# All additions of the last layer's pieces behind a block's edges, sums and shares in one PSUM tile, groups of four

## The chip, the cores and the metric

The kernel runs on one core of a Trainium2 chip, as one launch. The metric is the device time of one execution in microseconds (us). The core has five engines that run their own instruction streams and wait for each other through semaphores: TensorE (PE, matrix products; loads of its stationary operand appear as PEld), VectorE (DVE), ScalarE (ACT), GpSimd (POOL) and SyncE (SP, which here only issues transfers). Products land in PSUM, which has eight banks; all other tiles are in SBUF.

## The reference

The input is x (4096 x 128) and a sparse, symmetric pattern of edges in a dense matrix adj (4096 x 4096, float32, some ten entries a row, the diagonal among them, weights from 0.05 to 1). Four graph layers follow each other, each with a residual and a layer norm. The change concerns the last two:

```python
# layer 2: attention over the edges, 4 heads of 32 features
h_prime = (x @ weight.T).reshape(n, heads, f_out)
alpha_src = jnp.sum(h_prime * att_src, axis=-1)
alpha_dst = jnp.sum(h_prime * att_dst, axis=-1)
C = alpha_src[None, :, :] + alpha_dst[:, None, :]
adj_t = adj_matrix.T[..., None]
tau = adj_t * jnp.exp(jnp.maximum(0.2 * C, C))
tau_sum = jnp.sum(tau, axis=1, keepdims=True)
att_weights = tau / tau_sum
z = jnp.einsum('mnh,nhf->mhf', adj_t * att_weights, h_prime)
x = _layernorm(x + z.reshape(n, heads * f_out) + bias)
# layer 3: mean over the edges
deg = jnp.clip(jnp.sum(adj, axis=1, keepdims=True), 1.0)
h_neigh = adj @ h / deg
x = _layernorm(x + h @ W_self + h_neigh @ W_neigh)
```

## The kernel before

The layers ahead of these end with products of adj with dense blocks (L397, L687, L1685); beside them DVE and POOL build lists of each row's edges. `sparse_layers` (L1406) holds the two last layers. The 4096 rows are 32 blocks of 128 (NT = 32); adj is loaded as chunks of 1 MB, and columns of a product come in 8 stretches of 512 (NB = 8).

**Layer 2 for block t.** `gathers` (L1492) fetches the neighbours' rows from a table in DRAM with nine indirect transfers that POOL issues (L1497), two blocks ahead, into `got` (four buffers). Behind every second one stands a small POOL instruction, `pause` (L1391, L1393); two of the four read something and so wait: the second gather's reads `rd` of block t-2, the sixth's a column of the sum that was last added. `targets` (L1507) makes three small products that spread values of the target rows over the edges, in a PSUM tile `u` (shares, told[t]), one block ahead. `edges` (L1514) is DVE's work: `into` (L1523), scores (L1526 to L1529), an exponential on ACT (L1530), the weights (L1531, L1532, the latter written into `u`), the weighted rows `gw` (L1533) and the sum over the six near edges `here` (L1535). `sums` (L1538) adds up on PE in a PSUM tile `so`: three products with `into` and one of `here` with the identity (L1541, L1542). `divide` (L1545) divides by the sum of weights (`rd`, `z`) and adds to x; `turn` (L1555) transposes the block on PE and takes its statistics on DVE.

**Layer 3** is turned around: as soon as a group of n blocks has left layer 2, `layer3_rows` (L1562) makes its rows times both weight matrices (copy `oT` on ACT, n products L1575, then y and x scaled on ACT), and `layer3_product` (L1598) multiplies these rows with their part of adj: 8 stretches, each a product of n matmuls ("pieces") in a PSUM tile `pp`, to be added to the running sum `acc3` in SBUF by `add_up` (L1610; a copy on ACT for the first group, else an addition on DVE, L1618). The matrix part comes through `columns` (L1590) in 1 MB loads on SP's queue; five buffers hold them. `layer3_end` (L1620) does the last group together with the final norm and the store.

**The order** of PE, DVE, ACT and POOL is written out by hand: the loop over t near the end calls these functions in turn, `one(chains)` takes a step of `layer3_rows`, `one(pieces)` one matmul of `layer3_product`, and `multiply(n)` (L1667) up to n of these, with an `add_up` ahead of each, or, with held=True, without additions until two products wait. Each engine executes its instructions in exactly the order in which they are recorded.

PSUM before: two banks for `u`, three for `pp`, two for `px` (transposes, L1575), one for `so`. Groups are of 1, 1, fourteen times 2, 1 and 1 blocks.

Of the kernel before, what the change touches and what calls it, by code (L numbers as in the profile page):

```python
# [11 lines left out]
F32 = mybir.dt.float32  # L12
# [4 lines left out]
AF = mybir.ActivationFunctionType  # L17
ALU = mybir.AluOpType
AX = mybir.AxisListType
PSUM = bass.MemoryType.PSUM  # L20

P = 128
IB = 512
TB = IB // P
# [11 lines left out]
QT = 3  # L36
# [7 lines left out]
def adj_resnorm_d4(ctx: ExitStack, tc: tile.TileContext, x_in, xT_in, adj, adjT, w0g, w0gT, a0, w1a, b1a,  # L44
# [7 lines left out]
    nc = tc.nc  # L52
    N, F = x_in.shape
    NT = N // P
# [4 lines left out]
    H = att_src.shape[1]  # L59
# [11 lines left out]
    x = state.tile([P, NT, F], F32, name="x")  # L71
# [14 lines left out]
    eps = const.tile([P, 1], F32, name="eps")  # L86
# [1317 lines left out]
            nc.vector.tensor_tensor(flag, pb, flag0, ALU.add)  # L1404

    def sparse_layers(enter, lists, w, h0T):  # L1406
        psum, ps_p, ps_x, ps_so = [enter(name=n, bufs=b, space=PSUM) for n, b in (("ps_u", 2), ("ps_p", 3), ("ps_x", 2), ("ps_so", 1))]
        l2 = enter(name="l2", bufs=2)
        spread, table = lists.spread, lists.table
        lists.psum = psum  # L1410
        E = NEAR + QT
        W = 3 * H + 1
# [10 lines left out]
        def inverse(s, v):  # L1423
            nc.scalar.activation(s, v, AF.Sqrt, bias=eps)
            nc.vector.reciprocal(s, s)
# [63 lines left out]
        got, told, wide = {}, {}, {}  # L1489
        warm = small.tile([P, 1], F32, name="warm")  # L1490
# [16 lines left out]
        def targets(t):  # L1507
            if t < NT:
                at = wide[t // TB][:, t % TB]
                told[t] = psum.tile([P, QT * W + E * H], F32, name="u")  # L1510
                for j in range(QT):
                    nc.tensor.matmul(told[t][:, j * W:(j + 1) * W], at[:, j * P:(j + 1) * P], dst[:, t], start=True, stop=True)

        def edges(t):  # L1514

            g, u = got.pop(t), told.pop(t)
            d = u[:, 0:QT * W].rearrange("p (j s) -> p j s", s=W)
            wt = u[:, QT * W:].rearrange("p (j h) -> p j h", h=H)
            a = lists.value[:, t][:, :, None].to_broadcast([P, E, H])
            gw = l2.tile([P, E + 1, F + H], F32, name="gw")  # L1520
            nc.scalar.copy(gw[:, E, :], own[:, t, :])
            into = l2.tile([P, QT, P], F32, name="into")
            nc.vector.tensor_tensor(into, lists.iota[:, None, :].to_broadcast([P, QT, P]),  # L1523
                                    d[:, :, 3 * H:W].to_broadcast([P, QT, P]), ALU.is_equal)
            e = l2.tile([P, E, H], F32, name="score")
            nc.vector.tensor_reduce(e[:, 0:QT], d[:, :, 0:3 * H].rearrange("p j (s h) -> p j h s", s=3), AX.X, ALU.add)  # L1526
            nc.vector.tensor_tensor(e[:, QT:], g[:, QT:, F:F + H], near[:, t, :][:, None, :].to_broadcast([P, NEAR, H]), ALU.add)
            nc.vector.tensor_tensor(e[:, 0:QT], e[:, 0:QT], g[:, 0:QT, F:F + H], ALU.add)
            nc.vector.scalar_tensor_tensor(e, e, ALPHA, e, op0=ALU.mult, op1=ALU.max)  # L1529
            nc.scalar.activation(e, e, AF.Exp)  # L1530
            nc.vector.tensor_tensor(gw[:, 0:E, F:F + H], e, a, ALU.mult)  # L1531
            nc.vector.tensor_tensor(wt, gw[:, 0:E, F:F + H], a, ALU.mult)  # L1532
            nc.vector.tensor_tensor(heads(gw[:, 0:E, 0:F]), heads(g[:, :, 0:F]), wt[:, :, :, None].to_broadcast([P, E, H, FO]), ALU.mult)  # L1533
            here = l2.tile([P, F + H], F32, name="here")
            nc.vector.tensor_reduce(here, gw[:, QT:, :].rearrange("p j f -> p f j"), AX.X, ALU.add)  # L1535
            return into, gw, here

        def sums(into, gw, here):  # L1538
            so = ps_so.tile([P, F + H], F32, name="so")
            for j in range(QT):  # L1540
                nc.tensor.matmul(so, into[:, j, :], gw[:, j, :], start=j == 0, stop=False)  # L1541
            nc.tensor.matmul(so, ident, here, start=False, stop=True)  # L1542
            return so
# [18 lines left out]
        def layer3_rows(t0, n):  # L1562

            s = small.tile([P, n], F32, name="rstd2")
            xb = l2.tile([P, n, P], F32, name="oT")
            nc.scalar.copy(xb, turned.pop(t0))
            inverse(s, mv[:, t0:t0 + n, 1])
            yield
            qs = []
            for k0 in range(0, n, 2):  # L1570
                m = min(2, n - k0)
                q = ps_x.tile([P, m, 2, F], F32, name="px")
                qs += [(k0 + k, q[:, k]) for k in range(m)]
                for k in range(m):
                    nc.tensor.matmul(q[:, k].rearrange("p s f -> p (s f)"), xb[:, k0 + k, :],  # L1575
                                     W3.rearrange("p s f -> p (s f)"), start=True, stop=True)
            yield
            for k, q in qs:
                nc.scalar.activation(y[:, t0 + k, 0:F - 1], q[:, 0, 0:F - 1], AF.Copy, scale=s[:, k:k + 1])  # L1579
            for k, q in qs:  # L1580
                if n == 1:
                    nc.vector.tensor_scalar_mul(x[:, t0 + k, :], q[:, 1, :], s[:, k:k + 1])
                else:
                    nc.scalar.activation(x[:, t0 + k, :], q[:, 1, :], AF.Copy, scale=s[:, k:k + 1])
            nc.scalar.activation(warm, eps, AF.Exp)
            yield

        adds = deque()
# [9 lines left out]
        def layer3_product(t0, n):  # L1598

            for ib in range(NB):  # L1600
                if ib % (TB // n) == 0:
                    a = columns(t0, n, ib)
                p = ps_p.tile([P, IB], F32, name="pp")
                for k in range(n):
                    nc.tensor.matmul(p, y[:, t0 + k, :], a[:, ib % (TB // n), k, :], start=k == 0, stop=k == n - 1)  # L1605
                    if k == n - 1:
                        adds.append((t0, p, slice(ib * IB, (ib + 1) * IB)))
                    yield

        def add_up():  # L1610
            while adds:
                t0, p, blk = adds.popleft()
                nonlocal summed
                summed = acc3[:, blk.start:blk.start + 1]
                if t0 == 0:
                    nc.scalar.copy(acc3[:, blk], p)
                else:
                    nc.vector.tensor_add(acc3[:, blk], p, acc3[:, blk])  # L1618
# [36 lines left out]
        with tc.manual_schedule(engines={mybir.EngineType.PE, mybir.EngineType.DVE, mybir.EngineType.Activation,  # L1655
# [3 lines left out]
            def one(queue, n=1):  # L1659
                while queue and n:  # L1660
                    r = next(queue[0], queue)
                    if r is not queue:
                        n -= 1
                    else:
                        queue.popleft()

            def multiply(n, held=False):  # L1667
                for _ in range(n):
                    if not held:
                        add_up()  # L1670
                    elif len(adds) > 1:
                        break
                    one(pieces)

            def begin(t0, n):
                pieces.append(layer3_product(t0, n))
                return
                yield

            for ib in range(NB):  # L1680
                p = ps_p.tile([P, IB], F32, name="pp")
# [15 lines left out]
            nc.vector.memset(y[:, :, F - 1], 1.0)  # L1697
            lists.check()
            targets(0)
            sizes = [1, 1] + [2] * 14 + [1, 1]  # L1700
            groups = [(sum(sizes[:i]), n) for i, n in enumerate(sizes)]
            of = {t: g for g in groups for t in range(g[0], sum(g))}
            for t in range(NT):
                t0, n = of[t]
                if t % TB == 1:
                    load_spread(t // TB + 1)
                targets(t + 1)
                multiply(2)
                one(chains)
                multiply(1)  # L1710
                add_up()
                multiply(4, held=True)
                made = edges(t)
                add_up()
                if t == t0 + n - 1:
                    nc.scalar.activation(warm, eps, AF.Sqrt)
                so = sums(*made)
                multiply(2, held=True)
                rd = divide(t, so)
                turn(t, t0, n)  # L1720
                if t == t0 + n - 1:
                    chains.append(layer3_rows(t0, n))
                    if t < NT - 1:
                        chains.append(begin(t0, n))
                for _ in range(3):
                    one(chains)
                    multiply(1)
                behind = {1: rd}
                if summed is not None:
                    behind[5] = summed  # L1730
                gathers(t + 2, behind)
            while chains or pieces:
                one(chains)
                multiply(2)
            add_up()
# [46 lines left out]
```

## Time and profile before

| | |
|---|---|
| median of three runs | 1786.98 us (1784.92 to 1793.05) |
| the profiled execution | 1788.24 us, its span 1786.4 us |
| granted TensorE clock, mean over the span | 0.957 |
| PE busy | 1645.1 us, 92% of the span |
| DVE busy | 1091.3 us, 61% |
| POOL busy | 436.2 us, 24% |
| ACT busy | 371.7 us, 21% |
| additions to acc3 on DVE (L1618) | 128, 682 ns each |
| pieces on PE (L1605) | 496 records, two for each matmul |
| gathers on POOL (L1497) | 288, 962 ns each |

Shares of the whole span hide the stages: up to about 1330 us the dense products keep PE full; the two last layers take from there to 1750 us, and the final norm the rest. The granted clock is the mean share of full speed that PE got in a stretch. In the order of time a line gives the start and the duration in us, the engine, the line, the operation and its tiles, xN for N merged instructions, and in brackets how long the engine had stood idle and what ended it. "issue" means that it waited for nothing that the profile shows. Durations are of one profiled execution.

### The profile page before, as it was taken

How to read it: one execution, taken by the hardware profiler on the slowest of the kernel's cores; microseconds unless marked ns; L12 is line 12 of the kernel's file. 1: busy time of each engine (PE TensorE's matmuls, PEld its weight loads, DVE VectorE, ACT ScalarE, POOL GpSimd, SP SyncE). 2: the span in 40 equal slices, each digit the busy share in tenths (PEclk: the TensorE clock that was granted, in tenths of full speed). 3: DMA queues.
4: the chain of work that ended last, by engine and by line, in shares of the span. 5: the costliest groups of instructions: out<-in, count | busy, mean ns of one | idle time of the engine just before them, and what ended most of it. 6: DMA issues, size and time to landing. Idle time of an engine off the chain costs nothing.

```text
span 1786.4 us, 15851 instructions
## 1 busy us (share of the span) xinstructions
PE 1645.1 (92%) x4968; PEld 771.8 (43%) x4968; DVE 1091.3 (61%) x3066; ACT 371.7 (21%) x664; POOL 436.2 (24%) x636
## 2 busy tenths in 40 slices
PE   7999999999999999999999999999965788887884
PEld 3344445444444444444444444444432333443443
DVE  6655447888877876767966421232334667666665
ACT  5865501100000110101000000121222221222224
POOL 0000000000000000000463543000008877777752
PEclk8999999999999999999999999999986899889898
DMA  9987665688888567766877778888874677667772
GB/s 383 367 322 288 234 222 180 245 328 299 294 303 304 212 242 259 252 213 245 291 258 284 272 273 296 298 296 291 300 203 109 203 246 242 212 214 226 233 185 64
DMA packets 95936, 455.05 MB, mean 255 GB/s; under 512 B 15585, under 2 KB 25826, under 8 KB 52962
## 3 DMA queue, kind: packets, MB, share of 16 engines
q1 hardware_dynamic: 74256, 422.93, 67.2%
q0 software_dynamic: 12288, 19.54, 4.4%
q10 hardware_dynamic: 9298, 11.47, 1.9%
q8 instruction: 41, 0.67, 0.1%
q14 instruction: 53, 0.43, 0.1%
HBM read 446.48 MB, written 7.41 MB: 254 GB/s over the span
## 4 chain that ended last, share of the span: by engine, by line
PE 77%; DVE 10%; DMA 5%; ACT 3%; issue 3%; POOL 2%; ACTq 0%; DVEq 0%; POOLq 0%; SPq 0%
PE pacc L687 35%; PE pp L1685 12%; PE pacc L397 11%; PE pp L1605 6%; DMA chunk<-in_adjT 2%; DVE gw L1533 2%; POOL got L1497 2%; PE pmm L716 2%; DVE here L1535 2%; PE px L1575 1%; PE pden L385 1%; DVE acc L1618 1%; PE ptr L397 1%; DMA got<-table,source 1%; PE ptr L155 1%
## 5 line engine op out<-in xcount | busy, mean ns | idle before, releaser
L1497 POOL DMA_INDIRECT got<-table,source x288 | 277.0, 962 | 311.7 <-issue 307.2
L1386 POOL DMA_INDIRECT value<-in_adjT,where x96 | 99.5, 1037 | 638.1 <-DVE bad L1314 526.4
L1605 PE MATMUL pp<-chunk,xT 128*128 128x512 f32 x496 | 247.3, 647 | 6.1 <-ACT xT L1579 5.9
L687 PE MATMUL pacc<-chunk,v 128*128 128x512 f32 x512 | 225.4, 595 | 0.0
L1685 PE MATMUL pp<-chunk,w 128*128 128x512 f32 x512 | 224.6, 592 | 0.0
L687 PE MATMUL pacc<-chunk,t 128*128 128x512 f32 x512 | 223.5, 592 | 0.0
L687 PE MATMUL pacc<-chunk,x 128*128 128x512 f32 x512 | 222.1, 592 | 0.0
L397 PE MATMUL pacc<-chunk,hw 128*128 128x512 f32 x408 | 188.0, 605 | 2.1 <-DVE numT L425 1.3
L1274 DVE MAX8 top<-chunk 128x8 f32<-128x512 f32 x224 | 143.9, 679 | 57.4 <-DMA chunk<-in_adjT 57.4
L1275 DVE FIND_INDEX8 at<-top,chunk 128x8 uint16<-128x512 f32 x224 | 151.1, 685 | 0.0
L687 PEld LDWEIGHTS pacc<-chunk,v 128*128 128x128 f32 x512 | 95.9, 190 | 117.0 <-issue 117.0
L687 PEld LDWEIGHTS pacc<-chunk,x 128*128 128x128 f32 x512 | 96.2, 190 | 115.8 <-issue 115.8
L687 PEld LDWEIGHTS pacc<-chunk,t 128*128 128x128 f32 x512 | 96.1, 190 | 115.3 <-issue 115.3
L1605 PEld LDWEIGHTS pp<-chunk,xT 128*128 128x128 f32 x496 | 98.2, 210 | 108.9 <-issue 90.7
L1685 PEld LDWEIGHTS pp<-chunk,w 128*128 128x128 f32 x512 | 95.1, 190 | 109.3 <-issue 108.6
L1618 DVE TENSOR_TENSOR acc<-pp,acc 128x512 f32<-128x512 f32 x128 | 84.8, 682 | 48.4 <-PE pp L1605 48.2
L397 PEld LDWEIGHTS pacc<-chunk,hw 128*128 128x128 f32 x408 | 74.5, 190 | 92.2 <-issue 86.0
L328 DVE TENSOR_SCALAR pos<-chunk 128x2048 bf16<-128x2048 f32 x66 | 80.4, 1222 | 48.1 <-DMA chunk<-in_adjT 43.5
L369 ACT ACTIVATE junk<-chunk 128x2048 fp8e4<-128x2048 f32 x51 | 97.4, 1910 | 26.9 <-DMA chunk<-in_adjT 26.5
L1249 POOL IOTA i<- 128x384 int32 (+3 forms) x4 | 1.0, 260 | 333.1 <-PE pden L385 319.1
L1541 PE MATMUL so<-gw,into 128*128 128x132 f32 x192 | 30.1, 295 | 34.3 <-DVE gw L1533 34.1
L1535 DVE TENSOR_REDUCE here<-gw 128x132 f32<-128x924 f32 x32 | 58.4, 1825 | 1.1
(305 smaller groups left out, 1649.1 us busy)
## 6 DMA issues: line engine op xcount, KB each, us to landing
chunk<-in_adjT SPq DMA_DIRECT2D x386, 1024.0 KB, 4.9
keep<-in_adjT SPq DMA_DIRECT2D x13, 1024.0 KB, 8.1
spread<-spread ACTq DMA_DIRECT2D x16, 384.0 KB, 4.1
got<-table,source POOLq DMA_INDIRECT x288
table<-rows ACTq DMA_DIRECT2D x8, 264.0 KB, 6.5
xT<-in_xT ACTq DMA_DIRECT2D x8, 256.0 KB, 8.1
out<-o SPq DMA_DIRECT2D x8, 256.0 KB, 2.3
value<-in_adjT,where POOLq DMA_INDIRECT x96
```

Of the source, the lines that this page charges most:

```text
L328: r = nc.vector.tensor_scalar(pos, a, 0.0, None, op0=ALU.is_gt)
L369: nc.scalar.activation(junk, a, AF.Relu, scale=-1.0, accum_out=bad[:, n:n + 1], saturate=False)
L397: in_order(nc.tensor.matmul(p, hw[:, j * TB + k, :], a[:, k, :], start=first and k == 0, stop=last and k == TB - 1))
L687: nc.tensor.matmul(p, stationary(c * TB + k), a[:, k, :], start=n == 0 and k == 0, stop=n == NB - 1 and k == TB - 1)
L1274: nc.vector.max(self.top[:, t, ib, :], row)
L1275: nc.vector.max_index(self.at[:, t, ib, :], self.top[:, t, ib, :], row)
L1386: pin(nc.gpsimd.indirect_dma_start(self.value[:, c * TB + k, j:j + 1], None, flat, bass.IndirectOffsetOnAxis(ap=self.where[:, c * TB + k, ...
L1497: nc.gpsimd.indirect_dma_start(got[t][:, j, :], None, table, bass.IndirectOffsetOnAxis(ap=lists.source[:, t, j:j + 1], axis=0))
L1535: nc.vector.tensor_reduce(here, gw[:, QT:, :].rearrange("p j f -> p f j"), AX.X, ALU.add)
L1605: nc.tensor.matmul(p, y[:, t0 + k, :], a[:, ib % (TB // n), k, :], start=k == 0, stop=k == n - 1)
L1618: nc.vector.tensor_add(acc3[:, blk], p, acc3[:, blk])
L1685: nc.tensor.matmul(p, w[:, c * TB + k, :], a[:, k, :], start=c == 0 and k == 0, stop=c == NB - 1 and k == TB - 1)
```

## The change

The additions to acc3 no longer stand between the pieces. `multiply` issues up to n matmuls and stops when four products wait for their addition; `add_up` is called once a block, right behind `edges`, so that DVE adds up to four products in a row between `here` and `rd`. To hold four waiting products `pp` gets four banks; the bank comes from `so`, whose sums now lie in the same PSUM tile as the shares of the block (`u`, behind them). Groups become 1, 1, 2, four times 4, five times 2, 1 and 1. Six pieces stand ahead of the edges of a block and two behind its sums. In `layer3_rows` the load of the exponential's table (`warm` with Exp) moves ahead of the products of L1575, the product of the group is queued as soon as its y is there (before by a chain of its own, `begin`), and the scaling of x follows a step later, always on ACT. After the last block the rest of the pieces run with an `add_up` ahead of each two.

```diff
--- before.py
+++ after.py
@@ -1404,7 +1404,7 @@
             nc.vector.tensor_tensor(flag, pb, flag0, ALU.add)
 
     def sparse_layers(enter, lists, w, h0T):
-        psum, ps_p, ps_x, ps_so = [enter(name=n, bufs=b, space=PSUM) for n, b in (("ps_u", 2), ("ps_p", 3), ("ps_x", 2), ("ps_so", 1))]
+        psum, ps_p, ps_x = [enter(name=n, bufs=b, space=PSUM) for n, b in (("ps_u", 2), ("ps_p", 4), ("ps_x", 2))]
         l2 = enter(name="l2", bufs=2)
         spread, table = lists.spread, lists.table
         lists.psum = psum
@@ -1507,7 +1507,7 @@
         def targets(t):
             if t < NT:
                 at = wide[t // TB][:, t % TB]
-                told[t] = psum.tile([P, QT * W + E * H], F32, name="u")
+                told[t] = psum.tile([P, QT * W + E * H + F + H], F32, name="u")
                 for j in range(QT):
                     nc.tensor.matmul(told[t][:, j * W:(j + 1) * W], at[:, j * P:(j + 1) * P], dst[:, t], start=True, stop=True)
 
@@ -1515,7 +1515,7 @@
 
             g, u = got.pop(t), told.pop(t)
             d = u[:, 0:QT * W].rearrange("p (j s) -> p j s", s=W)
-            wt = u[:, QT * W:].rearrange("p (j h) -> p j h", h=H)
+            wt = u[:, QT * W:QT * W + E * H].rearrange("p (j h) -> p j h", h=H)
             a = lists.value[:, t][:, :, None].to_broadcast([P, E, H])
             gw = l2.tile([P, E + 1, F + H], F32, name="gw")
             nc.scalar.copy(gw[:, E, :], own[:, t, :])
@@ -1533,10 +1533,9 @@
             nc.vector.tensor_tensor(heads(gw[:, 0:E, 0:F]), heads(g[:, :, 0:F]), wt[:, :, :, None].to_broadcast([P, E, H, FO]), ALU.mult)
             here = l2.tile([P, F + H], F32, name="here")
             nc.vector.tensor_reduce(here, gw[:, QT:, :].rearrange("p j f -> p f j"), AX.X, ALU.add)
-            return into, gw, here
-
-        def sums(into, gw, here):
-            so = ps_so.tile([P, F + H], F32, name="so")
+            return u[:, QT * W + E * H:], into, gw, here
+
+        def sums(so, into, gw, here):
             for j in range(QT):
                 nc.tensor.matmul(so, into[:, j, :], gw[:, j, :], start=j == 0, stop=False)
             nc.tensor.matmul(so, ident, here, start=False, stop=True)
@@ -1565,6 +1564,7 @@
             xb = l2.tile([P, n, P], F32, name="oT")
             nc.scalar.copy(xb, turned.pop(t0))
             inverse(s, mv[:, t0:t0 + n, 1])
+            nc.scalar.activation(warm, eps, AF.Exp)
             yield
             qs = []
             for k0 in range(0, n, 2):
@@ -1577,12 +1577,11 @@
             yield
             for k, q in qs:
                 nc.scalar.activation(y[:, t0 + k, 0:F - 1], q[:, 0, 0:F - 1], AF.Copy, scale=s[:, k:k + 1])
+            if t0 + n < NT:
+                pieces.append(layer3_product(t0, n))
+                yield
             for k, q in qs:
-                if n == 1:
-                    nc.vector.tensor_scalar_mul(x[:, t0 + k, :], q[:, 1, :], s[:, k:k + 1])
-                else:
-                    nc.scalar.activation(x[:, t0 + k, :], q[:, 1, :], AF.Copy, scale=s[:, k:k + 1])
-            nc.scalar.activation(warm, eps, AF.Exp)
+                nc.scalar.activation(x[:, t0 + k, :], q[:, 1, :], AF.Copy, scale=s[:, k:k + 1])
             yield
 
         adds = deque()
@@ -1664,18 +1663,11 @@
                     else:
                         queue.popleft()
 
-            def multiply(n, held=False):
+            def multiply(n):
                 for _ in range(n):
-                    if not held:
-                        add_up()
-                    elif len(adds) > 1:
+                    if len(adds) > 3:
                         break
                     one(pieces)
-
-            def begin(t0, n):
-                pieces.append(layer3_product(t0, n))
-                return
-                yield
 
             for ib in range(NB):
                 p = ps_p.tile([P, IB], F32, name="pp")
@@ -1697,7 +1689,7 @@
             nc.vector.memset(y[:, :, F - 1], 1.0)
             lists.check()
             targets(0)
-            sizes = [1, 1] + [2] * 14 + [1, 1]
+            sizes = [1, 1, 2] + [TB] * 4 + [2] * 5 + [1, 1]
             groups = [(sum(sizes[:i]), n) for i, n in enumerate(sizes)]
             of = {t: g for g in groups for t in range(g[0], sum(g))}
             for t in range(NT):
@@ -1705,23 +1697,18 @@
                 if t % TB == 1:
                     load_spread(t // TB + 1)
                 targets(t + 1)
-                multiply(2)
-                one(chains)
-                multiply(1)
-                add_up()
-                multiply(4, held=True)
+                multiply(6)
                 made = edges(t)
                 add_up()
+                one(chains)
                 if t == t0 + n - 1:
                     nc.scalar.activation(warm, eps, AF.Sqrt)
                 so = sums(*made)
-                multiply(2, held=True)
+                multiply(2)
                 rd = divide(t, so)
                 turn(t, t0, n)
                 if t == t0 + n - 1:
                     chains.append(layer3_rows(t0, n))
-                    if t < NT - 1:
-                        chains.append(begin(t0, n))
                 for _ in range(3):
                     one(chains)
                     multiply(1)
@@ -1730,6 +1717,7 @@
                     behind[5] = summed
                 gathers(t + 2, behind)
             while chains or pieces:
+                add_up()
                 one(chains)
                 multiply(2)
             add_up()
```

## The prediction

> **What bounds the kernel now.** I read the page first for the share of each engine, then the stretches of 50 us for the stage that the change touches, then the chain that ended last in a part of that stage, and last the order of time on POOL and DVE. The stage runs from the first gather at 1336.2 us to the last addition at 1750.1 us: 32 blocks, each with 9 gathers on POOL, DVE's work on the edges, PE's sums, and a part of the last layer's products.
>
> ```profile
> 1486.00:1536.00 50.00, 41.64 (x121) 20.66 (x120) 33.09 (x74) 10.86 (x28) 38.07 (x53) 0.86 0.71 224
> 1536.00:1586.00 50.00, 41.61 (x122) 20.22 (x121) 33.70 (x76) 10.86 (x28) 38.04 (x53) 0.90 0.72 227
> 1586.00:1636.00 50.00, 41.03 (x123) 20.01 (x122) 33.74 (x76) 10.86 (x28) 37.92 (x52) 0.90 0.72 228
> ```
>
> After the length come busy time of PE, PE's weight loads, DVE, ACT and POOL, the granted clock and the DMA share. No engine is full: PE 83%, POOL 76% and DVE 67%. So the engines wait for each other in turn, and the chain says how.
>
> ```profile
> 1570.81 0.38 ACT xT L1579
> 1571.23 5.67 PE pp L1605 x8
> 1576.89 0.68 PE so L1541 x6
> 1577.57 0.48 PE so L1542 x2
> 1578.06 1.72 PE pp L1605 x4
> 1579.89 2.58 PE pp L1605 x6
> 1582.52 2.69 PE pp L1605 x6
> 1585.85 0.54 DVE into L1523
> ```
>
> The reader is to see that the edges of a block (from L1523) start only when DVE has added products that PE has just made. POOL is not in this chain; it waits for it:
>
> ```profile
> 1678.85 0.32 POOL L1393 TENSOR_TENSOR idle<-rd,idle 128x1 f32<-128x1 f32 x1
> 1692.06 0.19 POOL L1393 TENSOR_TENSOR idle<-rd,idle 128x1 f32<-128x1 f32 x1 [1.44 <-DVE rd L1548]
> 1704.03 0.31 POOL L1393 TENSOR_TENSOR idle<-rd,idle 128x1 f32<-128x1 f32 x1
> 1717.23 0.19 POOL L1393 TENSOR_TENSOR idle<-rd,idle 128x1 f32<-128x1 f32 x1 [1.43 <-DVE rd L1548]
> 1574.49 0.94 POOL L1497 DMA_INDIRECT got<-table,source  x1 [0.30 <-issue]
> 1575.81 0.98 POOL L1497 DMA_INDIRECT got<-table,source  x1 [0.15 <-issue]
> ```
>
> Two blocks take 1717.23 - 1692.06 = 25.2 us, 12.6 each. POOL alone needs less: early in the stage the same instruction stands at 1385.15 and 1396.84 with no wait, 11.69 us for nine gathers of some 1.25 to 1.3 us and four pauses. That is the stage's **floor**, and I ask whether the change reaches it.
>
> **The change, part by part.**
>
> *The floor and what it is worth.* The pause that waits for rd inside block 4's gathers ran at 1385.15. With no later wait, block 31's would run at 1385.15 + 27 x 11.69 = 1700.8, against 1717.23 now. From there the last seven gathers take 9.3 us (1704.03 to 1713.3 one block earlier), and their rows are usable 1.6 us after the last ends (block 0: gather ended 1347.6, L1527 began 1349.22). So the scores of block 31 can start at 1711.7. From there DVE takes 4.5 us to the end of here (1736.57 to 1741.07 now), then four additions at 0.65 (1.28 for two), so rd comes at 1711.7 + 4.5 + 2.6 = 1718.8. It came at 1742.19: **23.4 us earlier**, because DVE was also 8 us behind the gathers at the end.
>
> *Can PE and DVE keep up, groups of two?* The order of the changed program per pair of blocks is: 3 products, sums, 2, turn, 3; then 3, sums, 2, turn, 1, two of L1575, 2. A product matmul takes 0.86 (14 records, so seven of them, in 6.25 us less the tail). DVE's block without waits: edges 5.1 (1560.78 to 1565.92), four additions 2.6, rd to the statistics 1.3, together 9.0. The wait of 3.74 us that L1531 now has once a pair (the exponential stands on ACT behind y, x and a table load of 1.28) shrinks, as table load and x are no longer ahead of it, to about 2. A pair: 2 x 9.0 + 2 = 20, against 23.4 from POOL. It keeps up.
>
> *Groups of four.* Order: 6 products, sums, 2, turn, 3 in the first two blocks; 6, 2, 1 in the third; none in the fourth, then four L1575, one product. Blocks two and three are PE's: 11 x 0.86 + targets 0.25 + sums 0.97 + turn 0.14 = 10.8 each. The fourth is DVE's: 1.3 + 5.1 + ident product and latency 0.7 + one addition 0.65 + rd = 8.0. The first carries the chain: rd to x 0.85, turn 0.35, copy of oT 0.7, four L1575 at half clock 3.9 (two took 2.07 now), y 1.4, one product at half clock 1.7, targets 0.25, six products 6.0, sums 1.0: 16.2. Sum 45.8 against 4 x 11.69 = 46.8 from POOL. So the average just keeps up, and the first block overshoots by 4.5 us. That is allowed: at POOL's pause for rd of block t the gathers of t+1 ended 2.6 us before, so rd of t+1 can come 4.5 + 2.6 - 1.0 = 6.1 us after that pause, and POOL asks for it 11.7 after: 5.6 us of play.
>
> *The 32 additions fewer* (16 groups that DVE adds become 12; 128 additions become 96, and 32 x 0.68 = 21.8 us leave DVE). On the path this is worth what stands above and no more. If the play were gone, each addition behind an edge would cost its 0.65.
>
> *Sums in the shares' tile.* No instruction changes. PE's targets of t+1 now have to wait for z of t-1; turn of t-1 stands before them on PE and waits for x, which is later, so 0. Without that cover it would be up to the 0.3 us of z. rd now also waits for POOL's pause on its buffer three blocks before; that pause stands ahead of gathers that the same block needs, so 0.
>
> *ACT and SP.* 4 groups fewer save 8 table loads of 1.28; four x tiles move from DVE (0.35) to ACT (0.37). ACT is busy 22% of the stage: 0. SP issues 64 loads of 1 MB as before; for a group of four they are drawn by three blocks and none by the fourth. The mean is unchanged and five buffers cover it; the DMA share is 0.72. Bounds: from 0 to one landing time of 4.9 us a group, which the play takes up; I take 0.
>
> *The end.* Here the change pays back. The old order has 8 products behind the last sums, the new one 18. Old: rd 1742.19 to the first L1628 1749.19, 7.0 us. New: x 0.85, turn 0.2, one product 0.86, L1575 0.43, fifteen products 12.9: 15.2 us, 13 additions of 0.69 hidden behind them. **8.2 us later.** The last part (1749.19 to 1786.4, 37.2 us) is untouched.
>
> *Sum.* -23.4 + 8.2 = -15.2: a span of 1771.2 in place of 1786.4. The profiled execution took 1788.24 in all, 1.3 over the median of the runs, 1786.98. I set the difference against the median: **1772**.
>
> **The rivals.**
>
> *Half clock decides, slower.* PE does nothing but small work in the fourth block of each group, and an idle PE falls to half clock here: the four records of L1575 took 2.07 us at 1568.70 behind such waits, and 1.13 at 1420.61, at full clock; the windows above grant 0.86 to 0.90. I have put four L1575 and one product at half clock. If the six products ahead of the sums in the first block and in the second also ran so (12 x 0.86 = 10.3 more), a cycle would take 56.1 against 4 x 12.55 = 50.2 now. Four cycles lose 4 x 5.9 = 24, the ten blocks in pairs still gain about 8, the end costs 8: **1811**. It decides from 50.2 - 45.8 = 4.4 us of extra PE time a cycle. For it: PE's share in the cycle would be some 35 of 47 us, unevenly. Against it: now PE is back at full clock within 7 us of starting (0.86 per product again from 1575.4), with the same 25 us rhythm. The Trainium skill, "TensorE: Matmul & The Clock Gate", section "What's actually happening", has the clock halved after an idle window of about 3.4 us and restored after as long of steady work. By that rule each group pays one restart, as I count, and not the rival; the trace agrees, as 8 records took 5.67 and the next came at 0.43 each.
>
> *The play is too small, about the same.* Where the first block's overshoot exceeds 5.6 us, POOL waits as now. Two us in each of four cycles, and as much again in the early groups of one and two, bring rd of block 31 back by 10: **1782**. For it: 45.8 and 46.8 lie close, and the additions of up to four banks stand ahead of rd. Against it: in pairs 3.4 us of slack per pair give back a delay.
>
> *It does not bound at POOL, faster yet.* There is nothing under 11.69 in any row, so the floor holds to within the landing: at most 2 us better, inside my own range. The other way, gathers that land later beside bursts of 1 MB loads cost their delay once, at the end: 2 to 4 us, **1775**.
>
> **How the numbers follow.** Forecast (POOL's floor, longer end) 0.72, too little play 0.18, half clock 0.08, and 0.02 for what I don't see. Under 0.5% (9 us) this kernel's runs, which spread from 1784.92 to 1793.05, cannot be told from no change; so faster is under 1778, slower over 1796. The forecast lies in the first; the second rival mostly in "same"; some of the forecast's upper tail too. Faster 0.75, same 0.17, slower 0.08. The forecast's own range is 1766 to 1778: 5 below for the run's own spread, 6 above for late landings. To leave out no more than 2 in 10 I take 1765 to 1783.
>
> **What would show it.** Right: POOL's pause on rd runs every 11.7 us to the end with no wait on rd from the middle of the stage; L1527 waits for gathers in the groups of two; block 31's rd near 1719, the first L1627 near 1734; 96 additions; about 15 us of products behind the last block. Wrong: waits of POOL on rd of a us or more in each group of four; granted clock under 0.8 in the windows of groups of four; PE waiting on chunk loads; an rd period over 12 us.

## The result, and the profile after

The changed kernel takes **1775.55 us** (median of 7 runs, 1773.08 to 1783.17). The kernel before took 1786.98 (7 runs beside it, 1783.42 to 1793.05). The ratio is 0.9941, 95% interval [0.9919, 0.9964]: 11.4 us faster. In a second set of runs the same pair gave 0.9946 [0.9926, 0.9966], 1775.38 against 1787.65.

The first profiled execution happened to be the longest of its seven: 1783.17 us, a span of 1781.4. First the stretches of 50 us in the stage, with the same columns as before (length; busy time of PE, PE's weight loads, DVE, ACT, POOL; granted clock; DMA share; GB/s):

```profile
1486.00:1536.00 50.00, 40.65 (x127) 21.59 (x126) 31.20 (x72) 7.87 (x23) 40.50 (x58) 0.84 0.70 228
1536.00:1586.00 50.00, 40.21 (x124) 21.75 (x125) 29.78 (x71) 9.53 (x26) 40.58 (x55) 0.84 0.71 229
1586.00:1636.00 50.00, 49.02 (x156) 24.87 (x155) 30.48 (x69) 13.06 (x38) 40.55 (x58) 0.96 0.83 270
```

POOL is busy 40.5 us of 50 in place of 38.0, and the same in every stretch, while PE swings between 40 and 49 and DVE fell from 33.7 to about 30. 40.5 of 50 is POOL without waits: nine gathers of 0.962 us and four pauses of 0.205 are 9.5 us busy in a block of 11.67, and the rest is the 0.15 to 0.3 us that stands between one gather and the next. The order of time on POOL near the stage's end, with the four pauses of block 30 and the first of block 31's:

```profile
1691.23 0.20 POOL L1393 TENSOR_TENSOR idle<-rd,idle 128x1 f32<-128x1 f32 x1
1693.83 0.20 POOL L1393 TENSOR_TENSOR idle<-idle 128x1 f32<-128x1 f32 x1
1696.43 0.20 POOL L1393 TENSOR_TENSOR idle<-acc,idle 128x1 f32<-128x1 f32 x1
1699.04 0.20 POOL L1393 TENSOR_TENSOR idle<-idle 128x1 f32<-128x1 f32 x1
1702.89 0.20 POOL L1393 TENSOR_TENSOR idle<-rd,idle 128x1 f32<-128x1 f32 x1
```

No bracket stands behind the pauses on rd: the wait of 1.43 us is gone. From 1691.23 to 1702.89 it is 11.66 us, and all 29 distances between such pauses in this trace lie between 11.63 and 11.75. The chain of waits in the same stage has changed its character (start, length, what; pieces under 0.4 us are left out):

```profile
1563.16 0.98 POOL got L1497
1564.44 0.94 POOL got L1497
1565.76 0.98 POOL got L1497
1567.04 0.94 POOL got L1497
1568.35 0.98 POOL got L1497
1569.70 0.88 issue
1570.94 5.67 DMA got<-table,source
1578.26 1.36 DVE gw L1533
1579.65 1.83 DVE here L1535
1581.52 0.82 PE u L1541 x2
1583.32 0.49 PE px L1558
1583.83 0.59 ACT oT L1565
1584.47 3.78 PE px L1575 x8
1588.25 1.62 PE pp L1604 x2
1589.93 5.25 PE pp L1604 x12
```

Before, no line of POOL stood in this part of the chain. Now gathers follow one another in it, then the time until gathered rows are in place, then the edges. A piece of 5.67 us for those rows is new as well. The list of waits from 1360 us on says the same of DVE (total, times, longest):

```profile
DVE score L1527 <- DMA got<-table,source: 77.2, 24, 8.4
DVE rd L1547 <- PE u L1541: 18.6, 14, 2.7
DVE acc L1617 <- PE pp L1604: 5.6, 13, 1.0
```

L1527, the first work on a block's gathered rows, waits for them in 24 blocks. DVE waits only 5.6 us for products before it adds them; the 96 additions at L1617 are the 32 fewer that were announced. The end of the stage, in order of time:

```profile
1720.93 0.18 DVE L1527 TENSOR_TENSOR score<-got,near 128x24 f32<-128x24 f32 x1 [8.37 <-DMA got<-table,source]
...
1727.75 0.17 DVE L1547 RECIPROCAL rd<-u 128x4 f32<-128x4 f32 x1
...
1731.04 13.04 PE L1604 MATMUL pp<-chunk,xT 128*128 128x512 f32 x30
1743.92 0.39 PE L1627 MATMUL pp<-ident,acc 128*128 128x128 f32 x2
```

Here lies the loss of this execution. Its last gather ended at 1712.05, and block 31's score began 8.9 us later, after DVE had been idle 8.37 us for the rows. rd of block 31 came at 1727.75, 14.4 us earlier than before; then 30 records of products stand ahead of the last layer's end.

### The profile page after: what moved, and what is told of

Same layout as the page of the kernel before. It is cut to its first block, busy times and chain, and to the rows that moved or that the text cites. A ratio compares the mean times of both kernels' runs of the same rounds, so it can differ in the third digit from the quotient of the medians.

```text
span 1781.4 us, 15750 instructions
## 1 busy us (share of the span) xinstructions
PE 1637.1 (92%) x4968; PEld 775.7 (44%) x4968; DVE 1069.9 (60%) x3026; ACT 359.4 (20%) x644; POOL 435.2 (24%) x636
## 4 chain that ended last, share of the span: by engine, by line
PE 75%; DVE 7%; DMA 6%; POOL 6%; issue 3%; ACT 1%; ACTq 0%; DVEq 0%; POOLq 0%; SPq 0%
PE pacc L687 35%; PE pp L1677 12%; PE pacc L397 11%; POOL got L1497 6%; PE pp L1604 4%; DMA got<-table,source 3%; PE pmm L716 2%; DMA chunk<-in_adjT 2%; DVE gw L1533 1%; PE pden L385 1%; DVE acc L1617 1%; DVE here L1535 1%; PE ptr L397 1%; PE ptr L155 1%; PE px L1575 1%
## 5 line engine op out<-in xcount | busy, mean ns | idle before, releaser
L1540 PE MATMUL u<-gw,into 128*128 128x132 f32 x192 | 36.3, 337 | 68.4 <-DVE gw L1533 68.4
L1540 PEld LDWEIGHTS u<-gw,into 128*128 128x128 f32 x192 | 31.9, 235 | 83.1 <-DVE gw L1533 75.9
L1617 DVE TENSOR_TENSOR acc<-pp,acc 128x512 f32<-128x512 f32 x96 | 61.1, 680 | 5.6 <-PE pp L1604 5.6
```

## The experiments

They ran on three chips. On chip A the kernel before took 1787.65 us (11 runs, 1784.66 to 1790.47), on chip B 1866.42 (13 runs, 1857.32 to 1874.61), on chip C 1867.65 (15 runs, 1858.39 to 1881.06). Times are compared within a chip only; the four runs up to the additions between the products are from chip A. The chip of the first set above is not on record; its times are those of chip A. Each chip ran one set, so a difference between chips may also be one between moments. Diffs are against the changed kernel. "The theory" is that POOL's gathers set the pace of the stage.

### The changed kernel again

> The changed kernel, unchanged, profiled once more. Theory: POOL's pauses on rd stand 11.67 us apart from the third block on with no wait in every execution, and what differs between executions is how late the last gathers land (8.8 us behind the end of the last one in the profile shown, 1.6 us forecast) and the start of the stage. So a faster execution shows a landing of 2 to 6 us in block 31. Rival: the waits for gathers are the same and the 8 us between executions lie in the dense layers ahead of 1336 us.

1775.38 us (6 runs, 1773.25 to 1784.29). Its profiled execution, span 1772.4, ended the stage so:

```profile
1711.76 0.17 DVE L1527 TENSOR_TENSOR score<-got,near 128x24 f32<-128x24 f32 x1
...
1719.21 0.17 DVE L1547 RECIPROCAL rd<-u 128x4 f32<-128x4 f32 x1
...
1721.60 13.04 PE L1604 MATMUL pp<-chunk,xT 128*128 128x512 f32 x30
1734.48 0.38 PE L1627 MATMUL pp<-ident,acc 128*128 128x128 f32 x2
```

The last gather ended at 1709.46 and the score began 2.3 us later, not 8.9. No bracket stands behind the score: DVE did not wait for the rows, it came straight from block 30, whose rd was at 1709.33. So the rows had landed within 2.3 us. Of the 9.0 us between the two spans, 3.0 were there when the first gather started (1338.89 against 1335.91, so they come from the layers ahead), 6.6 lie between the last gather and the score, and 0.9 are the products at the end (16.2 against 15.3 us from rd to L1627). The small terms left over take 1.5 back.

### Groups of two throughout

```
-            sizes = [1, 1, 2] + [TB] * 4 + [2] * 5 + [1, 1]
+            sizes = [1, 1] + [2] * 14 + [1, 1]
```

> Groups as before (1, 1, fourteen of 2, 1, 1), all else as changed; 128 additions again. Theory (POOL's gathers bound the stage): pairs need 20 to 22 us from PE and DVE against 23.4 from POOL, so POOL still never waits for rd, and with 16 products behind the last sums in place of 18 the time is the changed kernel's within 2 us, about 1774. Rival (the 32 additions fewer are the gain): 32 x 0.68 = 22 us of DVE come back, half of them on the path: about 1785.

1775.01 us (5 runs, 1773.32 to 1778.88), 0.9935 [0.9922, 0.9948], with 128 additions again. POOL's pauses stand 11.63 to 11.73 us apart, without a wait on rd. So the groups of four and the 32 additions that they save are worth nothing that these runs can tell (0.4 us between the medians) beside a stage that POOL sets. One thing differs: with pairs DVE began on a block's rows 1.6 to 2.4 us after its last gather in 28 blocks of 32, with fours (the run above) in 14; the others took up to 6.1. With pairs the longest is the last block's: 4.2 us, and DVE did wait for the rows.

### The table load behind the scaling of x again

```
             inverse(s, mv[:, t0:t0 + n, 1])
-            nc.scalar.activation(warm, eps, AF.Exp)
             yield
...
-            if t0 + n < NT:
-                pieces.append(layer3_product(t0, n))
-                yield
             for k, q in qs:
                 nc.scalar.activation(x[:, t0 + k, :], q[:, 1, :], AF.Copy, scale=s[:, k:k + 1])
+            nc.scalar.activation(warm, eps, AF.Exp)
+            if t0 + n < NT:
+                pieces.append(layer3_product(t0, n))
             yield
```

> The exponential's table is loaded behind the scaling of x again, as before, and x is scaled in the same step as y; all else as changed. Theory: the exponential of the next block comes 2 to 3 us later once a group; in pairs 22 to 23 us stay under POOL's 23.4, in fours 45.8 + 3 us passes 46.8 by 2 in each of four cycles, part of which the play of 5.6 us takes: 1776 to 1784. Rival (the early table load is what gained, 14 groups x 1.9 us): back to 1786.

1777.1 us (5 runs, 1775.65 to 1780.63), 0.9945 [0.9932, 0.9957]. No wait of POOL on rd either. The median lies 1.7 us above the changed kernel's on this chip, which is within what the runs of either differ by. The theory's range was met at its lower end, but without the waits that it was built on; the rival, 1786, is out.

### Additions between the products, ahead of the edges

```
-            def multiply(n):
+            def multiply(n, held=False):
                 for _ in range(n):
-                    if len(adds) > 3:
+                    if not held:
+                        add_up()
+                    elif len(adds) > 1:
                         break
...
-                multiply(6)
+                multiply(3)
+                add_up()
+                multiply(4, held=True)
                 made = edges(t)
...
-                multiply(2)
+                multiply(2, held=True)
```

> Additions again ahead of every piece in front of the edges, and held at two behind them; groups, tiles and table load as changed. Theory: DVE reaches the edges only behind products that PE has just made, as before, 3 to 4 us later a block; blocks with seven products ahead of the edges take 13 us and more, over POOL's 11.67, and POOL waits on rd again: 1783 to 1793, with only 6 products left behind the last sums. Rival (POOL bounds whatever DVE does, the place of the additions does not matter): 1764 to 1768, as the end is 10 us shorter.

1823.62 us (5 runs, 1820.27 to 1827.32), 1.0201 [1.0186, 1.0215]: slower than the kernel before, and far past the range expected. Its waits and DVE's order of time show why:

```profile
DVE acc L1617 <- PE pp L1604: 131.7, 58, 8.1
```

```profile
1568.74 0.69 DVE L1617 TENSOR_TENSOR acc<-pp,acc 128x512 f32<-128x512 f32 x1 [2.10 <-PE pp L1604]
1572.34 0.69 DVE L1617 TENSOR_TENSOR acc<-pp,acc 128x512 f32<-128x512 f32 x1 [2.90 <-PE pp L1604]
1572.94 0.54 DVE L1523 TENSOR_TENSOR into<-iota,u 128x384 f32<-128x384 f32 x1
```

DVE must add before the edges may start, and in a group of four an addition is due only after four matmuls of 0.86 us: 3.4 us, which DVE spends waiting (131.7 us in place of 5.6). POOL then waits on rd 19 times, 38.1 us in all, rd of block 31 comes at 1776.79 in place of 1719.21, and 6 products at the end in place of 18 give back 7.5 us. So on this chip the gain hangs on the place of the additions: with the old place it is gone. Together with groups of four the old place is even worse than the kernel before, which had pairs; that the size of the groups makes this difference is worked out from the 3.4 us and was not run by itself. My expectation had counted the old waits of pairs.

### Additions also ahead of the block's six products

From here on the runs are from chips B and C; this one and the next are from B.

```
+                add_up()
                 multiply(6)
                 made = edges(t)
```

> As changed, with one more call of the additions per block, ahead of the six pieces (behind the targets). DVE then adds while it waits for gathers anyway, the pieces flow faster, and 6 products are left behind the last sums in place of 18. Theory (POOL bounds the stage, every product left behind costs its 0.86 us): 12 x 0.86 = 10.3 us less, of which 1 to 2 are given back because 8 products now stand ahead of the last sums on PE: 1766 to 1768, POOL still without waits on rd. Rival (the place of the additions is what gained; any addition ahead of the edges makes DVE wait for PE again): waits on rd come back and the time is 1780 or more.

1829.49 us (6 runs, 1827.88 to 1831.05), 0.9808 [0.978, 0.9836]. The expected times were made for chip A and cannot be held against chip B. The condition can: POOL did wait for rd, 15 times and 52.9 us in all, as the rival had it. The same with pairs:

> The same additional call, with groups as before (1, 1, fourteen of 2, 1, 1); 128 additions. Theory: as with groups of four, 6 products left behind the last sums, and gathers land at 1.7 us in nearly every block as in the other kernel with pairs: 1765 to 1768. Rival (with 32 additions more and additions ahead of the edges DVE is late): 1775 to 1780.

1829.73 us (6 runs, 1828.18 to 1831.71), 0.9809 [0.9781, 0.9837]. Fours and pairs are alike here too, and POOL waited with pairs as well (19 times, 51.9 us). Without a run of the changed kernel on that chip the ratio could not be taken apart, so the edit was run again beside it, with the two that follow.

### The changed kernel on chip C

> The changed kernel once more, beside the three that follow, so that all four are measured on one chip. Floor theory (POOL's nine gathers and four pauses set the stage): POOL's pauses every 11.7 us with no wait on rd, rd of block 31 near 1719, first L1627 15.3 us later, 0.994 to 0.996 of the kernel before. Rival (PE's products set the stage as soon as PE is slower than 0.86 us a product): POOL waits on rd in the groups of four, the stage is 30 to 50 us longer than in the first runs of the changed kernel, and so is the kernel before.

1842.68 us (6 runs, 1840.44 to 1843.57), 0.9858 [0.982, 0.9896]. This is what the rival said: POOL waits here, and the stage is long. The first gather starts at 1336.12 and the last part takes 36.9 us (37.9 on chip A); from the first gather to the first L1627 it is 467.9 us in place of 398.6, and the span is 1840.9. POOL's waits:

```profile
POOL idle L1393 <- DVE rd L1547: 56.1, 16, 10.5
```

In block 1 one sees where it starts. On chip C, with two lines of ACT that take products from PE ("remote" stands where the profile found no releaser):

```profile
1366.37 0.49 PE L1541 MATMUL u<-here,ident 128*128 128x132 f32 x2 [0.92 <-DVE here L1535]
...
1369.12 0.59 ACT L1615 COPY acc<-pp 128x512 f32<-128x512 f32 x1 [5.00 <-PE pp L1604]
...
1374.03 0.59 ACT L1615 COPY acc<-pp 128x512 f32<-128x512 f32 x1 [4.31 <-remote]
...
1376.93 0.18 DVE L1547 RECIPROCAL rd<-u 128x4 f32<-128x4 f32 x1 [10.62 <-remote]
```

and the same sums on chip A:

```profile
1366.22 0.49 PE L1541 MATMUL u<-here,ident 128*128 128x132 f32 x2 [0.92 <-DVE here L1535]
...
1366.75 0.18 DVE L1547 RECIPROCAL rd<-u 128x4 f32<-128x4 f32 x1 [0.58 <-PE u L1541]
```

The sums are recorded at the same time, but DVE stood idle 0.58 us for them on chip A and 10.6 us on chip C. Two copies that take earlier products stand 4.9 us apart there, where a product costs 0.86 us at full clock. So, by those who wait for them, PE's results come late in a way that its own records, whose ends are modelled, do not show. In all, rd waited 8 times without a recorded releaser on chip C, 37.0 us, and never so on chip A. What holds PE up is open. The queue for the chunk loads issued nothing between 1318 and 1374, and on chip B, in the run of eight gathers whose block 1 stalled alike, no packet of a chunk load moved from 1340 to 1370; so it is not these loads. On chip C no packet of an instruction queue moved from 1360 to 1378 either. And from 1366 to 1377 the granted clock in the records is 0.82 there, against 0.84 in the second execution on chip A, so the recorded clock does not explain it.

### Early additions, three banks and eight gathers beside it

Early additions, as above, on chip C:

> One more round of additions ahead of the block's six products, so that 6 products and not 18 stand behind the last sums. Floor theory: the stage stays at 11.7 us a block, the first L1627 comes 5.0 us after rd of block 31 and not 15.3, so 10 us under the changed kernel on the same chip: 1765 where that takes 1775. Rival (the additions ahead of the edges make DVE late for the gathers, as in the kernel before): POOL waits on rd a us or more in every second block, rd of block 31 comes 10 us later, and the time is that of the changed kernel or above.

1829.41 us (6 runs, 1827.13 to 1831.4), 0.9789 [0.9751, 0.9827], 13.3 us under the changed kernel, with ranges that do not touch. The theory was right on the end and wrong on the stage: POOL waited for rd 14 times (52.8 us), as it does in the changed kernel on this chip. The rival had those waits, but not the time. Next, three banks for the products:

```
-        psum, ps_p, ps_x = [enter(name=n, bufs=b, space=PSUM) for n, b in (("ps_u", 2), ("ps_p", 4), ("ps_x", 2))]
+        psum, ps_p, ps_x, ps_so = [enter(name=n, bufs=b, space=PSUM) for n, b in (("ps_u", 2), ("ps_p", 3), ("ps_x", 2), ("ps_so", 1))]
...
-                told[t] = psum.tile([P, QT * W + E * H + F + H], F32, name="u")
+                told[t] = psum.tile([P, QT * W + E * H], F32, name="u")
...
-            return u[:, QT * W + E * H:], into, gw, here
+            return ps_so.tile([P, F + H], F32, name="so"), into, gw, here
...
-                    if len(adds) > 3:
+                    if len(adds) > 2:
```

On chip B:

> Sums in a tile and bank of their own again and three banks for the products, so pieces stop when three wait for their addition; all else as changed. In pairs only 3 products a block can be made where 4 are needed, and 38 products are left behind the last sums in place of 18. Theory: POOL's 11.67 still bounds the blocks, and the end is 20 x 0.86 = 17.2 us longer: 1792 to 1794. Rival (the bank does not matter, the order does): 1775.

1853.98 us (8 runs, 1851.44 to 1856.13), 0.9935 [0.991, 0.996]. On chip C:

> The sums in a bank of their own again, three banks for the products and not four. Theory that the fourth bank lets PE run ahead of DVE within the floor: with three, at most three products stand ready behind each edge, PE falls behind by some products a block, 38 stand behind the last sums in place of 18: the first L1627 32 us after rd of block 31 in place of 15, so 17 us above the changed kernel, some 1792. Rival (the fourth bank is needed in the stage as well): POOL also waits on rd a us or more a block and rd of block 31 comes after 1730, so above 1800.

1854.51 us (10 runs, 1852.19 to 1858.52), 0.9928 [0.99, 0.9956], 11.8 us above the changed kernel. The ends of the three stages on chip C, the changed kernel first, then early additions, then three banks:

```profile
1788.76 0.17 DVE L1547 RECIPROCAL rd<-u 128x4 f32<-128x4 f32 x1
...
1791.16 13.04 PE L1604 MATMUL pp<-chunk,xT 128*128 128x512 f32 x30
1804.03 0.38 PE L1627 MATMUL pp<-ident,acc 128*128 128x128 f32 x2
```

```profile
1786.09 0.17 DVE L1547 RECIPROCAL rd<-u 128x4 f32<-128x4 f32 x1
...
1788.48 2.74 PE L1604 MATMUL pp<-chunk,xT 128*128 128x512 f32 x6
1791.06 0.38 PE L1627 MATMUL pp<-ident,acc 128*128 128x128 f32 x2
```

```profile
1783.06 0.17 DVE L1547 RECIPROCAL rd<-so 128x4 f32<-128x4 f32 x1
...
1785.46 30.20 PE L1604 MATMUL pp<-chunk,xT 128*128 128x512 f32 x70
1815.50 0.38 PE L1627 MATMUL pp<-ident,acc 128*128 128x128 f32 x2
```

The reader is to compare rd with L1627: 15.3, 5.0 and 32.4 us. Early additions save 10.3 us at the end as expected, and rd comes 2.7 us earlier on top. Three banks leave 17.1 us more products for the end, as expected, but rd comes 5.7 us earlier; that this is because fewer products stand ahead of the sums is argued, not shown. POOL waits as with four banks (15 times, 57.6 us, against 16 and 56.1). The fourth bank, with the shared tile that frees it, is worth the difference, 11.4 us of the 11.8 between the medians.

Last, eight gathers a block. The ninth neighbour's rows are a copy of the block's own, so this part of the result is left out:

```
+            nc.scalar.copy(got[t][:, E - 1, :], own[:, t, :])
-            for j in range(E):
+            for j in range(E - 1):
```

> Eight gathers a block: the ninth row's gather is left out and its place filled by a copy of the block's own rows on ACT (the sums are then not the reference's). Theory (POOL bounds, PE and DVE come right behind it, as worked out: 11.45 us a block in fours, 10 in pairs): POOL's floor falls to 10.4; blocks in fours go at 11.4 to 11.5, those in pairs at 10.4, waits of POOL on rd come back in the fours: 1750 to 1758. Rival (PE and DVE need as much as POOL anyway): 1768 or more, with waits on rd everywhere. Second rival (PE and DVE need far less): all blocks at 10.4, 38 us less, 1737.

1795.65 us (4 runs, 1793.98 to 1800.8), 0.9624 [0.9587, 0.966], on chip B. On chip C:

> Eight gathers a block in place of nine; the ninth neighbour's rows are not gathered but replaced by a copy of the block's own rows, so that part of the result is left out. Floor theory: the floor falls from 11.7 to 10.4 us a block, so the stage could end 40 us earlier, 1735 in all; but PE and DVE need 45.8 us for a group of four by the prediction, 11.45 a block, so POOL must now wait on rd, the stage ends 8 to 20 us earlier, and the time is 1755 to 1767. Rival (POOL was not the bound): no change beyond 3 us, with every pause of POOL later by the time saved.

1800.02 us (6 runs, 1795.06 to 1806.2), 0.963 [0.959, 0.967], 42.7 us under the changed kernel; I had expected the stage to end 8 to 20 us earlier. rd of block 31 comes at 1754.74 in place of 1788.76: 34.0 us over 32 blocks, 1.06 us a block, of the 1.3 that a gather takes. So on chip C, where POOL does wait on rd (61.1 us in 15 waits in this run), its gathers are none the less on the path. My reading, argued from the order of the program: the gathers behind a pause wait for rd, the next scores wait for those gathers, and the next rd for the scores. A wait of POOL in a profile did not mean that its work was covered. On chip A this run was not made; that POOL sets the pace there rests on its pauses, which never wait.

## Why the prediction came true, point by point

The forecast was a span of 1771.2 and 1772 us; measured were spans of 1772.4 and 1781.4, and medians of 1775.55 and 1775.38.

**The floor.** Right, and shown in both traces: 11.63 to 11.75 us from pause to pause, no wait on rd, where 11.69 was read from four early pauses. Block 31's pause was put at 1700.8 and ran at 1700.31 in the one and 1702.89 in the other. On chip C the floor is not reached, as PE's results come late. The change gains more there, 25 us against 11 to 12; that products made ahead cover late results is my reading, argued and not shown.

**Landing of the last rows.** This is the term that was mis-sized. It stood in the sum as 1.6 us, from block 0, where no chunk loads ran beside it. From the last gather to the score it measured 8.9 us in the first execution, 4.2 with pairs and 5.0 with the late table load, and DVE waited for the rows in all three; in the second execution it was 2.3, set by DVE and not by the rows. In the longer execution these stretches of 5 us show it (columns as above):

```profile
1705.00:1710.00 5.00, 4.04 (x15) 1.97 (x14) 4.96 (x6) 1.05 (x2) 4.06 (x7) 1.00 0.82 284
1715.00:1720.00 5.00, 1.96 (x5) 0.57 (x3) 0.00 (x0) 0.00 (x0) 0.00 (x0) 0.94 0.89 158
```

From 1715 to 1720 DVE, ACT and POOL do nothing at all; the DMA engines are busy 0.89 of the time, but move 158 GB/s where they moved 284 just before. The chunk loads there are those of the last groups, of one block each, in rows of 2 KB (361 packets for 0.71 MB); whether these small rows hold the gathers back is not shown. The third rival had this mechanism at 2 to 4 us and its time, 1775, is where the medians lie. That two profiles of the same kernel differ by 6.6 us at this place is shown; that every run's distance to the forecast is the same term is not.

**From score to rd.** 4.5 + 2.6 = 7.1 us were forecast; 7.45 (1711.76 to 1719.21) and 6.8 (1720.93 to 1727.75) came out.

**PE and DVE keep up.** Right in the first traces and on chip A, for twos and fours. The step that I put at 3.9 us, four L1575 at half clock at a group's start, took 3.78 in the chain above. The whole step, from the rd that ends a group of four to the next, was priced too high: 16.2 us forecast, 12.9 to 13.9 in the two traces. The sum had the 1.4 us of y on the path, but the product that follows the four L1575 is one left over from the group before and starts at 1588.05, while y is still being scaled; and six products took 5.25 us, not 6.0. So there was more play than the 5.6 us worked out. Within the groups of four one rd follows the other after 7.4 to 13.9 us; 14.9 and 15.2 come only in the pairs behind them in the first execution, in blocks 26 and 28, whose rows came 5.1 and 5.8 us after the last gather. POOL did not wait for any of this. On chip C they do not keep up.

**Fewer additions, the shared tile, ACT and SP.** All put at 0 on the path. For the additions and for ACT's order the runs with pairs and with the late table load agree. The shared tile itself brought no wait that a trace shows; the wait of rd for POOL's pause, also put at 0, came twice in the second execution, 0.7 us in all. But the bank that the shared tile frees is worth 11.8 us on chip C. I had it only as the reason why more products stand ready. On chip A three banks were not tried, so how much of the gain there is the bank's stays open. In the changed kernel DVE began on rows up to 6.1 us after their last gather inside the stage (second execution), and POOL still never waited: there such a delay is absorbed, and only the last block pays for it.

**The end.** 15.2 us from rd to L1627 were forecast, 15.3 and 16.2 measured, against 7.0 before. So the change pays back 8.3 to 9.2 us, forecast 8.2, and one more round of additions a block takes 10.3 of it away.

**The rivals.** Half clock did not decide: the windows grant 0.84 to 0.96 where they granted 0.86 to 0.90. The Trainium skill, "TensorE: Matmul & The Clock Gate", section "What's actually happening", has full clock come back within a few us of work. So it was in the chain above, where the first product after the slow L1575 took 1.62 us and the next six 0.88 each (5.25 for 12 records, two to a product). Too little play did not appear on chip A. Its sign, POOL waiting on rd in the groups of four, is what chip C shows, but with PE's results late, which the rival did not have.

**What it leaves.** The changed kernel with additions also ahead of the six products is the best version seen with the whole result: 0.9789 [0.9751, 0.9827] of the kernel before, where the changed kernel has 0.9858 [0.982, 0.9896]. It was run only on chips B and C; whether it gains its 10 us where POOL sets the pace stays open.

## What to carry to other kernels

Look for the engine that no row of the chain names but that waits a little in every turn: what it needs for one turn without waits is the floor, and a change is worth the distance to it, no more (here 23 us in the forecast, of which work pushed behind the last block took 8 back). An engine that consumes what another has just made should not stand ahead of the work that the loop turns on; put the consuming behind that work and give it buffers. And price the last turn apart from the others: delays that a steady loop absorbs (a landing, products left over) are paid in full there, once.

## What the runs showed of the hardware that I had not expected

One program, on different chips, needed the same time, within about 1 us, for its first 1336 us and its last 37, and 69 us more in between. It would be wrong to carry a gain in us, or the name of the engine that bounds, from one chip to the other: the ratio was 0.9946 [0.9926, 0.9966] on chip A and 0.9858 [0.982, 0.9896] on chip C.

PE's records can run ahead of PE: on chip C sums recorded at 1366.37 reached DVE at 1376.93. Whoever reads such a wait should look at who received the result, and when.

Where DVE stood waiting for the rows that POOL had gathered, it began on them 1.6 us after the last gather in block 0, with no chunk loads beside them, and up to 6.1 us after it in the stage of the changed kernel (second execution; 8.9 us once at the end of the first). With pairs throughout it was 1.6 to 2.4 us in 28 blocks of 32. Both kernels move the same bytes. The loads for groups of four come in rows of 8 KB and those for pairs in rows of 4 KB, but this alone does not explain it: in the changed kernel rows came late also beside the loads of the pairs, 5.1 and 5.8 us in blocks 26 and 28 of the first execution. The reason stays open.
